# Where the even chunk's values stand while the next unit's keys are projected

## The chip, the cores and the metric

The kernel runs on one core of one Trainium2 chip, in one launch. The metric is the time of one execution on the device in microseconds (us); the time before is the median of three runs.

The engines are named as the profile names them: PE is TensorE's matmul path and PEld its weight loads, DVE is VectorE, ACT is ScalarE, POOL is GpSimd, SP is SyncE, which here only issues DMAs.

## The reference

The reference is a block of three residual layers on x of 8 batches x 1024 tokens x 512 features, all in float32:

```
x = x + 0.5 * ffn(layernorm(x))      # 32 experts, each takes its 8 best tokens of a batch
x = x + attention(layernorm(x))      # the layer that the change is in
x = x + 0.5 * ffn(layernorm(x))
```

The attention has 16 heads of 32 features and is linear and causal:

```
q = exp(x @ Wq.T + bq);  k = exp(x @ Wk.T + bk);  v = x @ Wv.T + bv      # per head
kv = cumsum(k[:, :, None] * v[:, None, :], tokens);  k1 = cumsum(k, tokens)
out = einsum(q, kv) / sum(q * k1);  return out @ Wo.T + bo
```

## The kernel before, in words

**Stages.** The first feed-forward layer streams the experts' weights and lasts until about 820 us in the trace. The attention follows until about 1920, and then the second feed-forward layer streams its weights to the end.

**Tiling of the attention.** A batch has 8 chunks of 128 tokens (c); two chunks make a unit of 256 tokens (u). For batches 0 to 3 (NB0 = 4) the units are projected in the attention, by the generator `project` (L591). For batches 4 to 7 the projections were made beside the first feed-forward layer, and `project_rest` (L630) only scales and corrects them.

**What one unit's projection does.** `project` normalizes two chunks on DVE (L330), turns each with four PE transposes into a PSUM tile ps_aT (L338), and ACT copies each turned chunk to xnT (L339). Then 16 matmuls each form two key tiles ps_k (L610), ACT takes their exponential (L619), and `sum_keys` scans them along the tokens on DVE (L728). There it yields. The queries ps_q (the same lines) follow, and another yield; `times_keys` (L739, on POOL) is the last part.

**What one chunk does.** `attention` (L958) runs over batches and chunks and calls, for an even chunk of batches 0 to 3: `scores` (L785, masked by DVE at L796, by ACT and POOL at L801 and L803), `denominators` (PE L747 into ps_den, reciprocal on DVE L755), the first part of the next unit's projection, `values` (PE L819 into ps_v, copied to va by DVE L826), `turn_keys` (PE transposes L835 into ps_kt, copied to kc by ACT L837), `project_out` of the chunk before (PE L899, added by DVE L906), `spread_denominators` (PE L766), and `attend` (PE L849, L861 and L881). For an odd chunk the next part of the projection, the queries, comes ahead of its values. The values of a chunk read the xnT of that chunk's own unit; the keys at that place belong to the unit after it.

**What sets the order.** In the attention the instructions are recorded in the order of the calls, and a scheduler may move them on each engine; the order of each engine is then fixed, and an engine waits at an instruction until its semaphores are reached. The tiles ps_aT, ps_k, ps_q, ps_v, ps_kt, ps_den, ps_o, ps_n and those of the gate share the pool mm, which has three PSUM banks in the attention; a new tile waits until its bank's last reader has finished. Scores and the spread denominators have a pool of their own (sc).

**The gate.** While the chunks of one batch are worked on, the second layer's gate of the batch before is chosen on DVE in parts (L413 to L431, L518, L541); in the third chunk of batches 1 to 3 these stand among the projection's DVE work.

The lines that matter here:

```
            transposed(t, xnT[:, :, i * P : (i + 1) * P], xc, f"ps_aT_{b}_{c}")
        qkT = open_unit(t, s, b, u)
...
                    if (nb, nu) > (0, 1):
                        of = project_rest if rest else project
                        ahead = of(t, s, nb, nu) if nb < B else iter(())
                        next(ahead, None)
...
                if ("va", b, c) not in s:
                    values(t, s, b, c)
                if not rest:
                    turn_keys(t, s, b, c)
```

Of the kernel before, what the change touches and what calls it, by code (L numbers as in the profile page):

```python
# [20 lines left out]
def kernel(  # L21
# [60 lines left out]
    U = 2  # L82
# [246 lines left out]
    def normalize(dst, xt, mv, rs, c):  # L329
        nc.vector.tensor_scalar(  # L330
            dst, xt[:, c, :], mv[:, c, 0:1], rs[:, c : c + 1], ALU.subtract, ALU.mult
        )

    def transposed(t, dst, src, name):

        ps = t.mm.tile([P, NDC, P], F32, tag="mm", name=name)
        for dc in range(NDC):
            nc.tensor.transpose(ps[:, dc, :], src[:, dc * P : (dc + 1) * P], ident)  # L338
        nc.scalar.copy(dst, ps)  # L339
# [240 lines left out]
    def open_unit(t, s, b, u):  # L580

        un = t.un.tile([P, 4 * NDC * UT], F32, tag=f"un{u % 2}", name=f"un_{b}_{u}")
        qkT = un[:, : 2 * NDC * UT].rearrange("p (o n s) -> p o n s", n=2, s=UT)
        s["q", b, u], s["k", b, u] = qkT[:, :, 0, :], qkT[:, :, 1, :]
        s["k1", b, u], s["rr", b, u] = (
            un[:, i * NDC * UT : (i + 1) * NDC * UT].rearrange("p (o s) -> p o s", s=UT)
            for i in (2, 3)
        )
        return qkT

    def project(t, s, b, u, between=iter(())):  # L591


        xt, mv, rs = s["xt", b]
        xnT = t.n2.tile([P, NDC, UT], F32, tag="xnT", name=f"xnT_{b}_{u}")
        s["xnT", b, u] = xnT
        for i in range(U):
            c = u * U + i
            xc = t.n2.tile([P, D], F32, tag="xc", name=f"xc_{b}_{c}")
            normalize(xc, xt, mv, rs, c)  # L600
            nc.gpsimd.tensor_add(xt[:, c, :], xt[:, c, :], bo_sb)  # L601
            transposed(t, xnT[:, :, i * P : (i + 1) * P], xc, f"ps_aT_{b}_{c}")
        qkT = open_unit(t, s, b, u)
        for n, bias in (("k", bk_sb), ("q", bq_sb)):
            for oh in range(NDC // 2):
                ps = t.mm.tile([P, 2, UT], F32, tag="mm", name=f"ps_{n}_{b}_{u}_{oh}")
                for o in range(2):
                    oc = oh * 2 + o
                    for dc in range(NDC):
                        nc.tensor.matmul(  # L610
                            ps[:, o, :],
                            lhsT=w_sb[n][:, dc, oc * P : (oc + 1) * P],
                            rhs=xnT[:, dc, :],
                            start=(dc == 0),
                            stop=(dc == NDC - 1),
                        )
                for o in range(2):
                    oc = oh * 2 + o
                    nc.scalar.activation(  # L619
                        s[n, b, u][:, oc, :], ps[:, o, :], AF.Exp, bias=bias[:, oc : oc + 1]  # L620
                    )
                next(between, None)
            if n == "k":
                sum_keys(t, s, b, u)
                yield
        yield
        times_keys(t, s, b, u)
        yield
# [95 lines left out]
    def sum_keys(t, s, b, u):  # L724
        k1 = s["k1", b, u]
        before = s.pop(("k1", b, u - 1), None)
        for og in range(NDC):
            nc.vector.tensor_tensor_scan(  # L728
                k1[:, og, :],
                ones.to_broadcast([P, UT]),  # L730
                s["k", b, u][:, og, :],
                0.0 if before is None else before[:, og, UT - 1 : UT],
                ALU.mult,
                ALU.add,
            )

    def times_keys(t, s, b, u):
        qk = t.a1.tile([P, NDC, UT], F32, tag="qk", name=f"qk_{b}_{u}")
        nc.gpsimd.tensor_mul(qk, s["q", b, u], s["k1", b, u])  # L739
        s["qk", b, u] = qk  # L740
# [73 lines left out]
    def values(t, s, b, c):  # L814
        cols = slice(c % U * P, (c % U + 1) * P)
        va = t.a2.tile([P, D], F32, tag="va", bufs=3, name=f"va_{b}_{c}")
        ps = t.mm.tile([P, D], F32, tag="mm", name=f"ps_v_{b}_{c}")
        for dc in range(NDC):
            nc.tensor.matmul(  # L819
                ps,  # L820
                lhsT=s["xnT", b, c // U][:, dc, cols],
                rhs=w_sb["v"][:, dc, :],
                start=(dc == 0),
                stop=(dc == NDC - 1),
            )
        nc.vector.tensor_copy(va, ps)  # L826
        s["va", b, c] = va

    def turn_keys(t, s, b, c):

        cols = slice(c % U * P, (c % U + 1) * P)
        if c < NCH - 1:
            ps = t.mm.tile([P, NDC, P], F32, tag="mm", name=f"ps_kt_{b}_{c}")
            for og in range(NDC):
                nc.tensor.transpose(ps[:, og, :], s["k", b, c // U][:, og, cols], ident)  # L835
            kc = t.a2.tile([P, NDC, P], F32, tag="kc", name=f"kc_{b}_{c}")
            nc.scalar.copy(kc, ps)  # L837
            s["kc", b, c] = kc
# [119 lines left out]
    def attention(t, early, preload):  # L958
# [40 lines left out]
        for _ in project(t, s, 0, 0, begun):  # L999
            pass  # L1000
        ahead = project(t, s, 0, 1, begun)
        next(ahead)
        for _ in begun:
            pass
        last = None
        for b in range(B):
            for c in range(NCH):
# [16 lines left out]
                nb, nu = divmod(b * (NCH // U) + c // U + 1, NCH // U)  # L1024

                rest = NB0 <= nb < B
# [21 lines left out]
                if c % U == 0:  # L1048
# [21 lines left out]
# [3 lines that stand above are left out]
# [5 lines left out]
                    next(ahead, None)  # L1078
                if ("va", b, c) not in s:
                    values(t, s, b, c)  # L1080
                if not rest:
                    turn_keys(t, s, b, c)
                if last is not None:
# [479 lines left out]
    with ExitStack() as stack:  # L1563
        t = open_token_pools(stack, True, early, keep)
        attention(t, early, preload)
# [133 lines left out]
```

## Time and profile before

| what | us |
|---|---|
| median of three runs | 2563.76 |
| lowest and highest run | 2558.55, 2567.12 |
| the profiled execution, its own time | 2561.89 |
| the span of its trace, first to last instruction | 2560.0 |

| stage of the trace, us from its start | PE busy | DVE busy | DMA share |
|---|---|---|---|
| 0 to 830: first feed-forward layer | 741.1 of 830 | 190.2 | 0.96 |
| 904 to 1448: units projected in the attention | 532.5 of 544 | 253.4 | 0.07 |
| 1448 to 1780: units projected ahead | 313.2 of 332 | 246.7 | 0.34 |
| 1980 to 2560: second feed-forward layer | 334.8 of 580 | 48.2 | 0.96 |

A line of the timeline gives the start in us from the span's start, the duration, the engine, the line of the code, the operation with output and inputs, the tile's shape, and the number of instructions merged into the row. In brackets is the engine's idle time just before, and what released it. A wait is put down to the engine whose semaphore came last. The ends of matmuls are modelled, so the start of one group to the start of the next is the safer measure on PE. The granted clock is the share of TensorE's full clock that it was given.

### The profile page before, as it was taken

Reading aid. Unit: us, or ns where it says so; the run is one execution under the profiler, and the core shown is the slowest. Engines: PE = TensorE matmul, PEld = TensorE weight load, DVE = VectorE, ACT = ScalarE, POOL = GpSimd, SP = SyncE. Lnnn points to the kernel's source line nnn. Section 1 sums busy time; section 2 is a strip of 40 time slices with the busy share of each in tenths; the row PEclk is TensorE's granted clock in tenths of the full one; section 3 lists DMA queues with packets and bytes.
Section 4 is the critical chain, followed back from the end, with each engine's and each line's share of the span. In section 5 each row is a group of like instructions: output and inputs, shape, how many; then the busy total and the mean of one; then the engine's idle time right before and its main releaser. Section 6 shows DMA issues by size and latency. Waiting matters only on the chain.

```text
span 2560.0 us, 41819 instructions
## 1 busy us (share of the span) xinstructions
PE 2156.0 (84%) x18679; PEld 1134.8 (44%) x18679; DVE 867.4 (34%) x1495; ACT 498.2 (19%) x965; POOL 377.1 (15%) x345
## 2 busy tenths in 40 slices
PE   8799999999986999999999999999986555555555
PEld 5354544544532666666666655555541111110111
DVE  7311111111111343543544468878850000100002
ACT  6310001000000322322223233443530000000000
POOL 0000000000000112111112235545414000000002
PEclk9899999999997999999999999999987778878777
DMA  7799999999998000001010043243179999999995
GB/s 281 299 426 427 426 428 427 427 427 426 429 428 339 6 1 18 20 31 39 4 61 20 20 164 110 94 147 117 68 280 405 424 427 428 427 428 429 426 428 230
DMA packets 95636, 668.24 MB, mean 261 GB/s; under 512 B 18254, under 2 KB 22606, under 8 KB 58592
## 3 DMA queue, kind: packets, MB, share of 16 engines
q1 hardware_dynamic: 73952, 621.71, 58.9%
q10 hardware_dynamic: 18432, 35.66, 3.6%
q0 software_dynamic: 3072, 8.19, 0.8%
q8 instruction: 147, 2.41, 0.4%
q14 instruction: 33, 0.27, 0.0%
HBM read 614.34 MB, written 48.23 MB: 259 GB/s over the span
## 4 chain that ended last, share of the span: by engine, by line
PE 47%; issue 23%; DMA 16%; DVE 7%; ACT 2%; POOL 1%; POOLq 0%; ACTq 0%; DVEq 0%; SPq 0%
DMA w<-in_w 12%; PE ps_o L899 7%; PE ps_k L610 4%; PE ps_q L610 4%; PE ps_v L819 4%; PE ps_sq L1164 3%; PE ps_sk L1164 3%; PE h_ps L1254 3%; PE p_ps L1277 3%; PE sp L785 2%; PE ps_n L849 2%; DMA pg<-pmT_d,chosen_idx 2%; PE ps_sv L1181 2%; PE ps_n L861 2%; DVE st L314 1%
## 5 line engine op out<-in xcount | busy, mean ns | idle before, releaser
L1254 PE MATMUL h_ps<-w,mT 128*8 128x512 f32 x2048 | 285.9, 692 | 121.8 <-DMA w<-in_w 121.2
L1263 DVE STREAM_TRANSPOSE hs<-h_ps 128x512 f32<-128x512 f32 x64 | 45.9, 717 | 717.8 <-PE h_ps L1254 717.8
L1277 PE MATMUL p_ps<-w,pm 128*32 128x512 f32 x1024 | 173.6, 812 | 135.1 <-DMA w<-in_w 126.8
L899 PE MATMUL ps_o<-wo_sb,at 128*128 128x512 f32 x512 | 236.8, 606 | 1.1 <-ACT rsb L650 1.1
L1254 PEld LDWEIGHTS h_ps<-w,mT 128*8 128x8 f32 x2048 | 50.6, 94 | 332.0 <-issue 195.3
L1277 PE MATMUL p_ps<-w,gl 128*32 128x512 f32 x1024 | 132.5, 650 | 35.5 <-DMA w<-in_w 35.4
L601 POOL TENSOR_TENSOR xt<-xt,bo_sb 128x512 f32<-128x512 f32 x32 | 46.2, 1459 | 765.3 <-PE ps_ocT L338 706.1
L1277 PEld LDWEIGHTS p_ps<-w,pm 128*32 128x32 f32 x1024 | 35.3, 130 | 272.8 <-issue 130.7
L803 POOL TENSOR_SCALAR_AFFINE_SELECT am<-am 128x512 f32<-128x512 f32 x128 | 78.7, 639 | 436.0 <-ACT am L801 291.4
L899 PEld LDWEIGHTS ps_o<-wo_sb,at 128*128 128x128 f32 x512 | 93.5, 192 | 109.2 <-issue 103.4
L314 DVE BATCH_NORM_STATS2 st<-xt 128x6 f32<-128x512 f32 x192 | 128.3, 684 | 4.9 <-DMA xt<-in_x 2.4
L610 PE MATMUL ps_k<-xnT,wk_sb 128*128 128x256 f32 x512 | 115.3, 383 | 10.8 <-ACT xnT L339 10.8
L1270 ACT ACTIVATE pm<-a 128x128 f32<-128x128 f32 x32 | 9.9, 309 | 583.3 <-DVE a L1265 583.3
L1164 PE MATMUL ps_sq<-xcT,wq_sb 128*128 128x256 f32 x512 | 118.6, 388 | 4.1 <-ACT xcT L241 4.1
L1164 PE MATMUL ps_sk<-xcT,wk_sb 128*128 128x256 f32 x512 | 117.4, 385 | 0.0
L1181 PE MATMUL ps_sv<-wv_sb,xcT 128*128 128x512 f32 x256 | 115.6, 599 | 0.0
L819 PE MATMUL ps_v<-wv_sb,xnT 128*128 128x512 f32 x256 | 115.1, 593 | 0.0
L610 PE MATMUL ps_q<-xnT,wq_sb 128*128 128x256 f32 x512 | 115.1, 382 | 0.0
L1164 PEld LDWEIGHTS ps_sq<-xcT,wq_sb 128*128 128x128 f32 x512 | 96.7, 193 | 35.3 <-issue 17.4
L1164 PEld LDWEIGHTS ps_sk<-xcT,wk_sb 128*128 128x128 f32 x512 | 96.8, 192 | 28.0 <-issue 15.4
L610 PEld LDWEIGHTS ps_k<-xnT,wk_sb 128*128 128x128 f32 x512 | 95.8, 190 | 28.4 <-ACT xnT L339 14.6
L610 PEld LDWEIGHTS ps_q<-xnT,wq_sb 128*128 128x128 f32 x512 | 95.9, 190 | 15.7 <-ACT un L619 0.8
(246 smaller groups left out, 2835.3 us busy)
## 6 DMA issues: line engine op xcount, KB each, us to landing
w<-in_w SPq DMA_DIRECT2D x256, 2048.0 KB, 29.3
xt<-in_x SPq DMA_DIRECT2D x31, 1024.0 KB, 8.9
pre<-ahead_d SPq DMA_DIRECT2D x16, 1536.0 KB, 6.4
ahead_d<-ahead_qk ACTq DMA_DIRECT2D x16, 1024.0 KB, 11.5
out<-xt SPq DMA_DIRECT2D x16, 1024.0 KB, 4.7
xs<-in_x ACTq DMA_DIRECT2D x16, 512.0 KB, 18.2
ahead_d<-ahead_v ACTq DMA_DIRECT2D x16, 512.0 KB, 11.3
pm<-pm SPq DMA_DIRECT2D x16, 128.0 KB, 2.4
```

Source lines behind the costliest of these rows:

```text
L314: nc.vector.bn_stats(st, xt[:, c, :])
L610: nc.tensor.matmul(ps[:, o, :], lhsT=w_sb[n][:, dc, oc * P : (oc + 1) * P], rhs=xnT[:, dc, :], start=(dc == 0), stop=(dc == NDC - 1),)
L785: nc.tensor.matmul(sp[r // 2][:, r % 2, og, :], lhsT=kT[hr, og, cols], rhs=qT[hr, og, cols], start=True, stop=True,)
L803: nc.gpsimd.affine_select(out=am[1][:, i, :, :], in_=am[1][:, i, :, :], pattern=[[0, NDC], [1, P]], compare_op=ALU.is_ge, fill=0.0, base=0 ...
L819: nc.tensor.matmul(ps, lhsT=s["xnT", b, c // U][:, dc, cols], rhs=w_sb["v"][:, dc, :], start=(dc == 0), stop=(dc == NDC - 1),)
L849: nc.tensor.matmul(ps[hr, og, :], lhsT=va[:, (og * HG + r) * HD : (og * HG + r + 1) * HD], rhs=am[r // 2][:, r % 2, og, :], start=(og == 0 ...
L861: nc.tensor.matmul(ps[hr, og, :], lhsT=kv[hr, og, :], rhs=qT[hr, og, cols], start=False, stop=True, skip_group_check=True,)
L899: nc.tensor.matmul(ps, lhsT=at[:, oc, :], rhs=w_sb["o"][:, oc, :], start=(oc == 0), stop=(oc == NDC - 1),)
L1164: nc.tensor.matmul(ps[:, o, :], lhsT=w_sb[w][:, dc, oc * P : (oc + 1) * P], rhs=xcT[:, dc, :], start=(dc == 0), stop=(dc == NDC - 1),)
L1181: nc.tensor.matmul(ps, lhsT=xcT[:, dc, i * P : (i + 1) * P], rhs=w_sb["v"][:, dc, :], start=(dc == 0), stop=(dc == NDC - 1),)
L1254: nc.tensor.matmul(h[32 * j : 32 * j + B, :], lhsT=mT[:, dc, e, :], rhs=w1h[dc // 2][:, dc % 2, j * 512 : (j + 1) * 512], start=(dc == 0), ...
L1277: nc.tensor.matmul(pp[32 * j : 32 * (j + 1), :], lhsT=gl4[e % 4][:, q, :, :].rearrange("p i b -> p (i b)"), rhs=w2h[q // (NU // 2)][:, q % ...
```

## The change

`project` gets one more yield, between the turning of the tokens and the keys. Where the attention used to advance it once in an even chunk, it now advances it once before the values and once after them; ahead of the loop, the unit (0, 1) is advanced twice, so nothing moves there. For units projected ahead (`rest`) nothing changes. It concerns the units (0, 2) to (3, 3), 14 in all.

```diff
@@ project, after the turning of the unit's two chunks
             transposed(t, xnT[:, :, i * P : (i + 1) * P], xc, f"ps_aT_{b}_{c}")
+        yield
         qkT = open_unit(t, s, b, u)
@@ attention, ahead of the loop
         ahead = project(t, s, 0, 1, begun)
         next(ahead)
+        next(ahead)
         for _ in begun:
@@ attention, in the loop over chunks
                 if ("va", b, c) not in s:
                     values(t, s, b, c)
+                if c % U == 0 and not rest and (nb, nu) > (0, 1):
+                    next(ahead, None)
                 if not rest:
                     turn_keys(t, s, b, c)
```

## The prediction, made before the changed kernel ran

> **What bounds the kernel.** I read the page's busy times first, then a table of busy time by stage, then the waits of TensorE (PE) in the stage that the change touches, then the timeline of one unit there, engine by engine.
>
> ```profile
> PE 2156.0 (84%) x18679; PEld 1134.8 (44%) x18679; DVE 867.4 (34%) x1495; ACT 498.2 (19%) x965; POOL 377.1 (15%) x345
> ```
>
> The share over the whole span mixes stages, so the stage table decides. Its columns are the stretch and its length, busy time (and count) of PE, PEld, DVE, ACT and POOL, the granted PE clock, the DMA share and GB/s.
>
> ```profile
> 904.00:1448.00 544.00, 532.54 (x5229) 363.20 (x5230) 253.38 (x395) 148.22 (x276) 109.78 (x99) 1.00 0.07 23
> 1448.00:1780.00 332.00, 313.22 (x4346) 187.40 (x4348) 246.66 (x375) 131.43 (x254) 154.40 (x125) 0.97 0.34 117
> 1980.00:2560.00 580.00, 334.76 (x1936) 63.39 (x1928) 48.21 (x90) 8.35 (x27) 21.45 (x22) 0.78 0.96 405
> ```
>
> The 14 units that the change reorders are projected between 904 and 1448. There PE is busy 532.5 of 544 us at full clock, DVE 47% and DMA 7%: PE is the path, and only its 11.5 idle us can be won without removing work. The waits in that stage (who waited for whom: us in total, times, longest) say whose they are:
>
> ```profile
> PE ps_k L610 <- ACT xnT L339: 9.8, 14, 0.7
> PE ps_ocT L338 <- DVE oc L918: 1.7, 1, 1.7
> PE ps_aT L338 <- DVE xt L308: 0.9, 2, 0.7
> ```
>
> Fourteen waits, one for each reordered unit: the first key matmul waits for ScalarE (ACT) to copy the turned tokens out of PSUM. One unit on PE (start, duration, engine, line, what, count, idle before and its releaser):
>
> ```profile
> 1024.91 0.64 PE L747 MATMUL ps_den<-qk,hsum 128*32 128x256 f32 x8
> 1025.48 1.09 PE L338 MATMUL ps_aT<-ident,xc 128*128 128x128 f32 x8
> 1027.30 7.17 PE L610 MATMUL ps_k<-xnT,wk_sb 128*128 128x256 f32 x32 [0.73 <-ACT xnT L339]
> 1034.31 3.60 PE L819 MATMUL ps_v<-wv_sb,xnT 128*128 128x512 f32 x8
> 1037.74 0.60 PE L835 MATMUL ps_kt<-ident,un 128*128 128x128 f32 x4
> ```
>
> The reader is to see that the values (ps_v) stand behind the keys though they read the unit before (its xnT is long done). The same stretch on ACT and DVE:
>
> ```profile
> 1025.15 1.02 ACT L801 COPY am<-sp 128x1024 f32<-128x1024 f32 x1 [9.28 <-PE sp L785]
> 1026.17 1.07 ACT L339 COPY xnT<-ps_aT 128x512 f32<-128x512 f32 x2
> 1034.51 0.84 ACT L619 ACTIVATE un<-ps_k,bk_sb 128x256 f32<-128x256 f32 x2 [2.61 <-PE ps_k L610]
> ```
>
> ```profile
> 1026.15 1.75 DVE L755 RECIPROCAL rd<-ps_den 128x256 f32<-128x256 f32 x1
> 1037.94 0.69 DVE L826 COPY va<-ps_v 128x512 f32<-128x512 f32 x1 [1.53 <-PE ps_v L819]
> ```
>
> **The bubble's size.** PE's ends overlap what follows: four transposes (ps_kt) show 0.60 us, but the next group starts 0.44 after them. So the idle column is short by 0.16 each time, and the bubbles come to 9.8 + 14 x 0.16 = 12.0 us.
>
> **The change, part by part.** The order of instructions in the built program, with the waits that it carries, shows what moves. On PE, in 14 units, the four value matmuls stand ahead of the sixteen key matmuls; nothing else. On DVE the copy va (L826) stands ahead of the four scans (L728), in three units also ahead of L426, L431 and L518. The orders of ACT, POOL and SP are unchanged, so no DMA is issued earlier or later in its queue, and nothing is added or removed: busy time changes by 0.
>
> *When can the values start?* They need a PSUM bank of the three of pool mm, and in the built program their first matmul waits for ACT, one count short of what the first key matmul waits for: for the first of the two xnT copies, which frees the first transposes' bank. One copy lasts 0.586 us (minimum and median of its line), and before the change PE starts 0.05 after the second one's end (1026.17 + 1.07 = 1027.24, keys at 1027.30). So the values start where the first copy ends, and the gain of a unit is the duration shown for both copies less 0.59. I read the 14 pairs: seven show 1.07 us (0.48 each, 3.4), two 1.13 or 1.14 (0.55, 1.1), four 1.29 (0.70, 2.8). In the first unit (0, 2) the first copy has ended before the last transposes; these start at 906.08, take 0.44, and the keys started at 907.40, so 0.85 (less the 0.03 that I leave). **Sum: 8.1 us.** What stays is 12.0 - 8.1 = 3.9 us of waiting for the first copy.
>
> *What is late next?* The values take 3.43 us from start to start (1034.31 to 1037.74), the second copy ends 0.5 to 0.7 us after the values start, so the keys find it done: 0. The second key group takes the bank of the denominators, released by the reciprocal L755; it starts 3.43 + 3.5 us after the values, and the worst reciprocal ends 4.5 us after the old key start (unit 1233, below): 0. The turning of the keys (ps_kt) now takes the values' bank and waits for va. That copy is queued behind DVE's backlog, worst where the top-k of the gate runs:
>
> ```profile
> 1236.74 1.75 DVE L755 RECIPROCAL rd<-ps_den 128x256 f32<-128x256 f32 x1
> 1240.89 1.12 DVE L541 TENSOR_SCALAR chosen_idx<-chosen_idx 32x8 uint32<-32x8 uint32 x1
> 1241.93 1.21 DVE L426 SCALAR_TENSOR_TENSOR pm<-pm,lg 32x1024 f32<-32x1024 f32 x1
> ```
>
> There va takes L426's place at 1241.9 and ends at 1242.6; ps_kt comes at 1234.00 - 0.55 + 10.44 = 1243.9. Margin 1.3 us, so 0. If DVE were 2 us later, the three such units would lose 0.7 each, 2 us in all. Queued behind ps_kt on PE is the output projection, so such a wait would be paid in full.
>
> The later key exponentials come 3.43 us later against PE, and two scans with them. ACT then copies kc (L837) behind two exponentials (0.84), about 0.4 us later than now; its reader, the ps_kv matmuls, stand 6 us behind (1043.71). The scans end about 2.0 us after ps_kt starts; the next DVE work (L906) waits for the output projection 4.1 us after that start. Both are covered: 0. In the top-k units L906's margin is 1 us.
>
> *Does it reach the end?* Between 1448 and 1780 PE is still busy 94%, and the last stage runs on its weight stream (DMA 0.96), whose first big batch is issued at 1867 behind the attention's last batch. Everything after is released by work on this chain, so I carry it over in full.
>
> [...] The keys' start 0.05 us after the second copy is a data wait, since the copy writes what they read. [...]
>
> **The rivals.**
> - *Bank gap* (0.08): the values get no bank before the second copy, or the order on the chip is not that of the build. For: three banks only, all three drawn just before. Against: the wait on the first copy. 0 us: 2563.8.
> - *Whole bubble* (0.10): the values run straight behind the transposes. For: they have no data to wait for. Against: the same bank. -12.0: 2551.8.
> - *Given back* (0.16): PE meets a later wait, at ps_kt or L906 in the top-k units, or in the stages after 1448 where DVE is busy 74%. For: margins of 1.0 to 1.3 us. Against: those engines are released by PE itself. About half remains: -4, 2559.7.
> - *Slower: the bank of the denominators* (0.04). Three banks in plain rotation would hand the values the bank of ps_den, free when the reciprocal ends. It decides as soon as that end lies behind the old key start, and it does in all 14 units: by 0.6 (1027.90 against 1027.30) in six and 0.3 in the first, 2.3 in four, 3.8 and twice 4.5 in the top-k ones, in sum about 26 plus 0.05 for each: +26.7, 2590.5. Against: before the change the keys were next in that rotation, and started 0.6 us ahead of that end.
>
> **How the numbers follow.** The profiled execution took 2561.89 us, of which 2560.0 is the span; less 8.1 it would be 2553.8. The median of the three runs is 1.87 us above it, so the forecast stands at 2563.76 - 8.1 = **2555.7**, chance 0.62. The three runs spread by 8.6 us, and half-clock stretches (0.97 between 1448 and 1780) fall elsewhere in each execution; a median of three may be off by 3. The range 2550 to 2563 takes in that, the whole bubble and the bank gap. About 0.3% (7.7 us, below 2556.1) is what a measurement of this kernel can tell from no change, and my forecast lies right on it. So faster: 0.62 x 0.55 + 0.10 x 0.95 + 0.16 x 0.1 = 0.45; slower 0.04; the rest, 0.51, within.
>
> **What would show it.** The fourteen waits of ps_k on xnT vanish, and shorter ones of ps_v on xnT, 0 to 0.25 us, stand in their place; the values start 0.05 us after the first copy's end; from there to ps_kt stays 10.44 us; PE's idle time in the stage falls by 8. It is wrong if ps_v waits for DVE, if ps_kt waits for va, or if the stretch from 904 to the last unit shortens by 8 and the end does not.

## The result, and the profile after

The changed kernel takes 2555.22 us in the median of seven runs (2551.45 to 2559.55), the kernel before, run beside it, 2564.97 (2558.55 to 2568.60). The ratio is 0.9964, with a 95% interval of 0.9954 to 0.9974: 9.2 us faster (6.7 to 11.8); the two medians themselves lie 9.75 apart. Seven more runs of it later gave 0.9970 (0.9958 to 0.9981), 7.7 us. The forecast was 2555.7, or 8.1 us.

The busy times of the page of the changed kernel come first, then its table by stage. The columns are those of the tables of before.

```profile
PE 2165.0 (85%) x18679; PEld 1142.9 (45%) x18679; DVE 865.8 (34%) x1495; ACT 497.1 (19%) x965; POOL 373.8 (15%) x345
```

```profile
904.00:1440.00 536.00, 532.43 (x5224) 361.87 (x5225) 251.58 (x395) 145.64 (x272) 106.56 (x99) 1.00 0.07 23
1440.00:1772.00 332.00, 315.56 (x4349) 191.02 (x4347) 244.37 (x371) 129.57 (x251) 153.51 (x124) 0.96 0.33 114
```

The reader is to see that no engine has other work: the counts over the whole span are those of before. PE does the same 532.4 us in a stretch that is 8 us shorter. Over the whole span its busy time is 9.0 us more than before, with as many instructions; the granted clock is a half for 416.4 us of this execution and for 396.0 of the one before, so the sum over the span says nothing about the change. The PE waits from 880 to 1440 (who waited for whom: us in total, times, longest) say which idle time went:

```profile
PE ps_v L820 <- ACT xnT L339: 1.7, 7, 0.2
PE ps_ocT L338 <- DVE oc L919: 1.7, 1, 1.7
PE ps_aT L338 <- DVE xt L308: 0.9, 2, 0.7
```

The 14 waits of the keys (9.8 us) are gone, and seven short ones of the values stand in their place. The same unit as in the prediction, on PE, then on ACT and DVE:

```profile
1024.54 1.09 PE L338 MATMUL ps_aT<-ident,xc 128*128 128x128 f32 x8
1025.87 3.70 PE L820 MATMUL ps_v<-wv_sb,xnT 128*128 128x512 f32 x8 [0.24 <-ACT xnT L339]
1029.41 7.07 PE L611 MATMUL ps_k<-xnT,wk_sb 128*128 128x256 f32 x32
1036.32 0.60 PE L836 MATMUL ps_kt<-ident,un 128*128 128x128 f32 x4
```

```profile
1025.23 1.07 ACT L339 COPY xnT<-ps_aT 128x512 f32<-128x512 f32 x2
```

```profile
1029.61 0.69 DVE L827 COPY va<-ps_v 128x512 f32<-128x512 f32 x1 [1.82 <-PE ps_v L820]
1037.02 1.39 DVE L729 TENSOR_TENSOR_SCAN un<-ones,un,un 128x256 f32<-128x256 f32 x2 [1.99 <-ACT un L620]
```

One copy lasts 0.59 us, so the first ends at 1025.82. The values start at 1025.87; the second copy ends at 1026.31, three us ahead of the keys, which find it done. In 13 of the 14 units the values start 0.05 us after the first copy's end; in the first the copy is done before the last transposes, and the values follow these.

**One execution is a poor witness for the end.** The profiled executions took 2561.89 us before and 2559.55 after (the slowest of its seven), only 2.3 less. I split each trace at two starts of the turning of keys (ps_kt): the one just ahead of the 14 units (888.58 in the trace of before) and the one of the last unit's odd chunk (1473.23). The first two rows are of before, the other two of after:

```profile
888.58 0.60 PE L835 MATMUL ps_kt<-ident,un 128*128 128x128 f32 x4
1473.23 0.60 PE L835 MATMUL ps_kt<-ident,un 128*128 128x128 f32 x4
```

```profile
889.88 0.60 PE L836 MATMUL ps_kt<-ident,un 128*128 128x128 f32 x4
1466.14 0.60 PE L836 MATMUL ps_kt<-ident,un 128*128 128x128 f32 x4
```

Between them lies all that the change touches, and in what follows this is "the stage". It takes 584.65 us before and 576.26 after: 8.4 us less. The other 6.1 us were lost elsewhere: 1.3 ahead of it, where the attention began later, 3.8 between it and the last ps_kt (1875 before), and 0.9 behind. In the part with the 3.8 the instructions are the same, but the granted clock falls to a half in stretches of 3.4 us (half-clock stretches, below) that lie differently in each execution: from 1450.6 to 1872.5 they come to 20.5 us before and 30.7 after. A kernel whose 14 units run exactly as before (the sixth below) shows 37.5 us of them, and 5.3 us more in that part than the execution of before. In the ten traces kept here that part lasts from 402.1 us, where it has the least half clock (the 20.5 of before), to 409.5, where it has the most (41.0, kernel 2 once more). So the 3.8 need no cause in the change, and the runs together, which average over this, agree with the whole 8.4.

### The profile page after: what moved, and what is told of

The parts are those of the page before. It is cut to its first block, busy times and chain, and to the rows that moved or that the text cites. A ratio compares the mean times of both kernels' runs of the same rounds, so it can differ in the third digit from the quotient of the medians.

```text
span 2557.7 us, 41819 instructions
## 1 busy us (share of the span) xinstructions
PE 2165.0 (85%) x18679; PEld 1142.9 (45%) x18679; DVE 865.8 (34%) x1495; ACT 497.1 (19%) x965; POOL 373.8 (15%) x345
## 4 chain that ended last, share of the span: by engine, by line
PE 48%; issue 23%; DMA 16%; DVE 7%; ACT 1%; POOL 1%; POOLq 0%; ACTq 0%; DVEq 0%; SPq 0%
DMA w<-in_w 12%; PE ps_o L900 7%; PE ps_q L611 4%; PE ps_v L820 4%; PE ps_k L611 4%; PE ps_sk L1168 3%; PE ps_sq L1168 3%; PE h_ps L1258 3%; PE p_ps L1281 2%; PE ps_n L850 2%; PE ps_sv L1185 2%; PE sp L786 2%; DMA pg<-pmT_d,chosen_idx 2%; PE ps_n L862 2%; DVE st L314 1%
## 6 DMA issues: line engine op xcount, KB each, us to landing
ahead_d<-ahead_qk ACTq DMA_DIRECT2D x16, 1024.0 KB, 11.5
```

## The experiments

My theory after the result: the gain is made on PE alone; the values run while ACT makes the second copy, and what is left of the bubble is the wait for the PSUM bank that the first copy frees. The rivals: the gain comes from DVE, which copies the values ahead of the scans; it would come with any work put in the bubble; or the bubble was a lack of PSUM from the start. The table gives each kernel's ratio to the kernel before, run beside it; the difference that follows (the median of the kernel before, in that comparison, times the ratio less 1); the difference of the stage; and how many half-clock stretches of 3.4 us that stage has more than in the trace of before, which has two, at 896.5.

| kernel | ratio (95%) | us | stage, us | half-clock stretches more |
|---|---|---|---|---|
| changed kernel | 0.9964 (0.9954 to 0.9974) | -9.2 | -8.4 | 0 |
| changed kernel, once more | 0.9970 (0.9958 to 0.9981) | -7.7 | -8.4 | 0 |
| 1: copy of the values behind the scans | 1.0017 (1.0007 to 1.0028) | +4.4 | +5.5 | 1 |
| 2: values in the scores' bank | 0.9938 (0.9924 to 0.9951) | -15.9 | -14.4 | 0 |
| 2, once more | 0.9944 (0.9929 to 0.9960) | -14.4 | -11.4 | 2 |
| 3: denominators as the filler | 0.9994 (0.9981 to 1.0006) | -1.5 | +0.9 | 3 |
| 4: values in the denominators' bank | 1.0104 (1.0087 to 1.0121) | +26.7 | +26.7 | 7 |
| 5: scores' bank, copy behind the scans | 0.9961 (0.9948 to 0.9974) | -10.0 | -12.7 | 1 |
| 6: before, keys in the scores' bank | 1.0000 (0.9991 to 1.0009) | 0.0 | 0.0 | 0 |

The stage agrees with the medians to within 3 us in every row, and where the stretches are as many as before, to within 1.5. So what is gained or lost in the 14 units reaches the end, as far as these intervals, of 2 to 4 us to each side, can tell.

**1: DVE's copy put back behind the scans.**

```diff
-        nc.vector.tensor_copy(va, ps)
+        if late:
+            s["vp"] = va, ps
+        else:
+            nc.vector.tensor_copy(va, ps)
...
                 if c % U == 0 and not rest and (nb, nu) > (0, 1):
                     next(ahead, None)
+                if "vp" in s:
+                    tc.keep_in_program_order(nc.vector.tensor_copy(*s.pop("vp")))
```

> The changed kernel, with DVE's copy of the even values put back behind the four scans in the 14 units; PE keeps the new order, values ahead of keys. My theory: the 8 us come from PE, which runs the values while ACT makes the second copy of the turned tokens; DVE's order gains nothing. Then the keys still start about 3.4 us after the values and no wait on the turned tokens longer than 0.25 us comes back. The new order of DVE costs a little of its own: the turning of the keys takes the bank of the first keys, and the output projection waits for ACT's exponentials of the second keys, which end about 1.04 us after the turning starts, where PE is ready after about 0.77: 0.3 us in each of 14 units, +4 us on the changed kernel, so about 4 to 5 us below the kernel before (ratio 0.998). Rival: the gain comes from the copy standing ahead of the scans on DVE, and the kernel is back at the time of before (ratio 1.000 or above).

It came out 4.4 us slower than before. By the time alone this is the rival's ratio (1.000 or above), but the trace gives it another reason. The values start as in the changed kernel, their waits are the same 1.7 us in seven units, and 10.44 us later ps_kt starts. But behind that PE's order is another one: half of the spread denominators now stand ahead of the output projection. I put that down to the scheduler, which finds the bank of the values free later and the banks of pool mm in another rotation; no run shows that reason apart. Their group in the stretch from 904 to 1440 (busy us, mean ns of one, idle before), of the changed kernel and then of this one:

```profile
L767 PE MATMUL ps_rr<-rd,hrep 32*128 32x256 f32 x104 | 9.3, 427 | 0.0
```

```profile
L767 PE MATMUL ps_rr<-rd,hrep 32*128 32x256 f32 x104 | 18.2, 426 | 0.0
```

The same 104 matmuls, 13 units, occupy 8.9 us more, 0.68 a unit. Eight together take 0.65 us to the next group; two groups of four take 0.63 each (in the unit at 1038.34). Against the changed kernel the way from the even chunk's ps_kt to the next one is 0.81 us longer in eight units, 0.40 in two, 1.40 in three (in the one at 1037.81 the next scores are split too), and 2.39 in the last, into which a half-clock stretch at 1462.7 falls: 13.9 in all, as much as the stage lost. So the run spoke of PE's order, not of DVE's, and could not decide its question.

**5: the same question without the side effect.** With the values in the scores' bank (2, below) the copy can be put behind the scans and PE's order stays the same to the instruction. The diff is those of 1 and 2 together.

> The kernel with the values in the scores' bank, with one thing more: DVE copies the even values behind the four scans again, as before the change. The order of PE, ACT, POOL and SP is the same to the instruction as with the values in the scores' bank; only DVE's order differs. The run with the late copy in the old bank could not tell what DVE's order is worth, because its banks rotated differently and the spreading of the reciprocals and the scores were split on PE. My theory: the gain is made on PE alone; the copy ends about 2.8 us after the turning of the keys starts, the next reader of its bank comes 5.3 us after it, and DVE's next work waits for the output projection at 4.1: ratio 0.993 to 0.995, the same as with the early copy, and about 0.2% below the changed kernel. Rival: half or more of the gain came from the copy standing ahead of the scans: ratio 0.997 or above.

The stage gained 12.7 us where kernel 2 gained 14.4. Of the 1.7 between them, 1.5 come from a half-clock stretch at 1120.8 in the unit whose ps_kt starts at 1112.46 (23.92 us to the next ps_kt, where kernel 2 takes 22.45), 0.2 from everything else. So DVE's order is worth next to nothing, and the gain is PE's. The time itself (0.9961) is higher than I expected. Its interval begins at 0.9948, where those of kernel 2 lie from 0.9924 to 0.9960: by the time alone the two can't be told apart for sure, nor this one from the changed kernel. What the trace shows of the stage doesn't explain a difference of 4 to 6 us, so that part stays open (there were five runs).

**2: another bank for the values.**

```diff
-        ps = t.mm.tile([P, D], F32, tag="mm", name=f"ps_v_{b}_{c}")
+        if aside:
+            ps = t.sc.tile([P, 2, 512], F32, tag="sp1", name=f"ps_v_{b}_{c}")[:, 0, :]
+        else:
+            ps = t.mm.tile([P, D], F32, tag="mm", name=f"ps_v_{b}_{c}")
```

> The changed kernel, with the even values of the 14 units written to the second PSUM tile of the scores, which is free when ACT has copied the masked scores, ahead of the first copy of the turned tokens. My theory: what is left of the bubble in the changed kernel (3.9 us by the forecast's sum) is the wait for the bank that the first copy frees. With another bank the values start straight behind the turning, the waits of the values on the turned tokens go from 7 to about none, and the kernel is 3.5 to 3.9 us faster than the changed one: about 12 us, or 0.47%, below the kernel before (ratio 0.9953, where the changed kernel measured 0.9964). Rival: the values start 0.05 us after the first copy for another reason than the bank (PE's own latency behind the transposes, or data), and nothing changes against the changed kernel. Second rival: the second half of the reciprocals' spreading, which takes the scores' tile later in the unit, then waits for DVE's copy of the values; a wait of PE on that copy would show at its line and take the gain back.

It beats both kernels, by more than I expected. One unit on PE:

```profile
1022.28 1.10 PE L338 MATMUL ps_aT<-ident,xc 128*128 128x128 f32 x8
1023.21 3.60 PE L823 MATMUL ps_v<-wv_sb,xnT 128*128 128x512 f32 x8
1026.65 7.07 PE L611 MATMUL ps_k<-xnT,wk_sb 128*128 128x256 f32 x32
1033.56 0.60 PE L839 MATMUL ps_kt<-ident,un 128*128 128x128 f32 x4
```

The values follow the turning 0.93 us after its start, without a wait; in the changed kernel it was 1.33. From the values to ps_kt it takes 10.34 us, not 10.44 (1026.65 to 1033.56 is 6.91 in both; the values' own part is 3.44 instead of 3.54). A wait on PE thus cost 0.10 us more than its idle time here. (I call this the restart.) And in the first unit, whose two chunks are turned with a wait between them, the first two value matmuls run inside that wait, and its ps_kt comes 0.79 us sooner behind the one before it. So what was left in the changed kernel was 3.9 us of waiting, 1.3 of restarting (13 x 0.10) and 0.8 in the first unit: 6.0; the stage shows 14.4 - 8.4 = 6.0. The bank was the cause of all of it. No wait of PE on the copy va shows, so the second rival did not come true either.

> The kernel with the even values in the scores' bank once more, since it had five runs and its advantage over the changed kernel is 6 us or less of 2555. My theory: from the turning of the keys ahead of the 14 units to that of the last, it is 14.4 us shorter than the kernel before, as in its first trace, and all of it reaches the end: ratio 0.993 to 0.9955. Rival: its first ratio of 0.9938 was partly luck, and the version is no better than the changed kernel's 0.9964 to 0.9970.

The second time the ratio was 0.9944. The stage gained 11.4 us in that execution, with two more half-clock stretches in it (three instead of two at 895 to 905, and one at 1120.3), which at 1.5 us each bring back the 14.4. Both intervals lie almost wholly below the two of the changed kernel.

> The changed kernel itself once more, beside the two above on one chip, so that the bank's worth is read against it there. My theory: ratio to the kernel before 0.996 to 0.997, and in its trace the reciprocal of the last unit again 8 us earlier against that of the first than in the kernel before. Rival (part of the gain is given back behind the stage, as the single profiled execution seemed to say with 2.3 us): ratio 0.998 or above.

The stage gained 8.4 us again, to 0.1, and the end 7.7 by the ratio.

**3: another filler.**

```diff
                 if c % U == 0:
-                    if not rest:
+                    if not rest and (nb, nu) <= (0, 1):
                         denominators(t, s, b, c // U)
...
                 if c % U == 0 and not rest and (nb, nu) > (0, 1):
+                    denominators(t, s, b, c // U)
                     next(ahead, None)
```

It stands in the changed kernel with its values put back behind the keys.

> The kernel before with its values behind the keys, as before the change, but the eight matmuls of the denominators (0.57 us from start to start in the unit at 1024.91) put between the turning of the next unit's tokens and its keys in the 14 units. My theory: a filler gains only if the copies of the turned tokens don't shift with it. Here they do not start earlier when the transposes do, because ACT is still copying the masked scores until 1026.17 in that unit; PE comes to the turning 0.57 us sooner, waits for the same copies and finds the keys at the same time: 0 to -2 us against the kernel before (ratio 0.999 to 1.000). Rival: any work of PE in the bubble is won in full, 14 x 0.57 = 8 us (ratio 0.997). Second rival: the reciprocal on DVE starts 0.5 to 1 us later and what reads the denominators' bank, the second group of keys, waits for it in the three top-k units: +1 us each, +3 us.

No difference that can be measured. PE, ACT and DVE in the unit:

```profile
1026.86 1.09 PE L338 MATMUL ps_aT<-ident,xc 128*128 128x128 f32 x8
1027.88 0.64 PE L748 MATMUL ps_den<-qk,hsum 128*32 128x256 f32 x8
1029.14 7.17 PE L611 MATMUL ps_k<-xnT,wk_sb 128*128 128x256 f32 x32 [0.62 <-ACT xnT L339]
```

```profile
1027.10 1.01 ACT L802 COPY am<-sp 128x1024 f32<-128x1024 f32 x1 [9.28 <-PE sp L786]
1028.01 1.08 ACT L339 COPY xnT<-ps_aT 128x512 f32<-128x512 f32 x2
```

PE turns the tokens earlier, but ACT is still copying the masked scores. The copies keep their place behind that, and the keys start 0.05 us after the second, as before. The 0.57 us put into the bubble had stood ahead of the turning, beside the same copy of the scores, and PE waits on as before. From each ps_kt of the 14 units to the next it takes 0.1 to 0.4 us less than before, 2.3 us in the twelve intervals without a half-clock stretch: a third of the 12 x 0.57 that the rival promised. The stage came out 0.9 longer because three such stretches fell into it, two in the first unit (the clock is a half until 911.3 there, and until 903.3 in the trace of before) and one at 1293.6. The second rival, keys waiting for a later reciprocal, didn't show. So not any filler did: work from ahead of the turning won these 2.3 us, and work from behind the keys won 8.4 (the changed kernel), which is 0.60 a unit, the time of a copy.

**4: the slower rival, built.**

```diff
-        ps = t.mm.tile([P, UT], F32, tag="mm", name=f"ps_den_{b}_{u}")
+        both = s["both"] = t.mm.tile([P, D], F32, tag="mm", name=f"ps_den_{b}_{u}")
+        ps = both[:, :UT]
...
-        ps = t.mm.tile([P, D], F32, tag="mm", name=f"ps_v_{b}_{c}")
+        if shared:
+            ps = s["both"]
+        else:
+            ps = t.mm.tile([P, D], F32, tag="mm", name=f"ps_v_{b}_{c}")
```

> The changed kernel, with the even values of the 14 units written into the PSUM tile of the denominators, so that they must wait for DVE's reciprocal. One key matmul stands ahead of them on PE. This builds the slower rival of the forecast to see whether its mechanism and price are real. By that sum each unit stalls until the reciprocal's end: against the kernel before, about 0.2 us in six units, 1.9 in four, 3.4 and twice 4.1 in the top-k ones, +20 us (about 2584, ratio 1.008), with waits of the values on DVE of that sum in the trace of PE. Rival: DVE's reciprocal moves up with PE, since it waits for the denominators and not for DVE's backlog, and the price is under half of that (ratio below 1.004).

The values bear the name ps_den here. Their wait from 904 to 1475, and one unit with the gate's top-k:

```profile
PE ps_den L824 <- DVE rd L757: 14.5, 7, 3.4
```

```profile
1241.03 1.13 PE L611 MATMUL ps_k<-xnT,wk_sb 128*128 128x256 f32 x4 [0.68 <-ACT xnT L339]
1245.57 6.66 PE L824 MATMUL ps_den<-wv_sb,xnT 128*128 128x512 f32 x8 [3.41 <-DVE rd L757]
1252.06 6.21 PE L611 MATMUL ps_k<-xnT,wk_sb 128*128 128x256 f32 x28
```

The mechanism is real: PE waits for the reciprocal in the seven units where it ends late (1.26 us four times, 2.70 once, 3.41 twice). In the other seven the key matmul in front, four rows of 0.97 us together, covers it, more than the 0.44 that I had allowed. A unit with a wait of 1.26 and a full clock takes 1.52 us longer than before, which is the wait, the 0.16 of the modelled ends and the 0.10 of a restart. The waits and seven times 0.26 come to 16.3 us, under my 20. The rest is something I had not counted: eight value matmuls take 6.49 us to the next group here (1245.57 to 1252.06), against 3.44 without a wait. The granted clock (0.50, behind the busy times of PE, PEld, DVE, ACT and POOL) is a half there:

```profile
1244.72:1251.55 6.83, 5.99 (x7) 2.52 (x8) 6.45 (x9) 1.24 (x2) 3.77 (x2) 0.50 0.00 0
```

In or just behind five of the seven waits there are such stretches, seven of 3.4 us in all, and they are left with 26.7 - 16.3 = 10.4 us, 1.5 each.

**6: was it PSUM from the start?**

```diff
-                ps = t.mm.tile([P, 2, UT], F32, tag="mm", name=f"ps_{n}_{b}_{u}_{oh}")
+                if n == "k" and oh == 0 and (b, u) > (0, 1):
+                    ps = t.sc.tile([P, 2, 512], F32, tag="sp1", name=f"ps_{n}_{b}_{u}_{oh}")
+                    ps = ps[:, 0, :].rearrange("p (o s) -> p o s", s=UT)
+                else:
+                    ps = t.mm.tile([P, 2, UT], F32, tag="mm", name=f"ps_{n}_{b}_{u}_{oh}")
```

This is the kernel before with that edit alone.

> The kernel before with one thing changed: the first key group of the 14 units is written to the second tile of the scores, which is free before the turned tokens are copied. The order on all engines is that of before. This asks whether the 12 us in front of the keys were a wait for PSUM. My theory: it is a wait for data, since the keys read what the second copy writes; the bank changes nothing, the waits of the keys on the turned tokens stay at 9.8 us in 14 units, ratio 0.999 to 1.001. [...]

Nothing moved, and the wait is the old one to the digit:

```profile
PE ps_k L614 <- ACT xnT L339: 9.8, 14, 0.7
```

The bank itself was free: in kernel 2 the values run in it from 1023.21, before the first copy has ended (1022.98 + 0.59 = 1023.57). So the keys waited for data. The other bank helped only where something without that data stood in front: by 14.4 us of the stage in kernel 2, by 0.0 here.

## Why the prediction was right

- **What bounds.** Right. PE's idle time in the stretch fell from 11.5 to 3.6 us, by 7.9 where 8 was forecast, and the busy time stayed.
- **When the values start.** Right: 0.05 us after the first copy in 13 units. The pairs of copies gave 7.3 for these 13, and from ps_kt of the first unit to that of the last the trace is 7.33 us shorter. The first unit gave 1.05, forecast as 0.82. Sum 8.1, measured 8.4 in two traces.
- **What is late next.** Right. ps_kt comes 10.44 us behind the values. In the top-k units of the changed kernel va ends 1.2 us ahead of it (1239.13 against 1240.30); I had said 1.3. L906 (now L907), whose margin I gave as 1 us, cost nothing either.
- **Does it reach the end.** Right over all runs. My own test for it (the stretch shortens by 8 and the end does not) would have condemned it from the one trace; it should have asked for the medians. That the median, 2555.22, lies 0.5 us from the forecast is in part luck: the kernel before came out 1.2 us above the three runs that I had started from, and the interval of the gain is 2.6 us to each side. No run shows the 0.3% (7.7 us) that my chances took as what a measurement can tell from no change; seven runs of each kernel left 2.6 us, 0.1%, to each side.
- **The bubble's size.** Too small. I had 12.0, from idle time and 0.16 for each end. The rival that fills it whole is worth 14.4 us, not 12.0, because a restart costs 0.10 a unit (1.3) and the first unit offers more than I had counted: 0.2 of it in the changed kernel, 0.8 with the free bank.
- **The slower rival.** Its price of 26.7 is what kernel 4 shows, but by chance: its units lose 16.3 by waiting, and the lowered clock, which my sum did not have, makes up the rest.
- **The gap's cause.** I had taken the gap for a data wait, and what the change leaves of it for a wait for a bank. Kernel 6 (ratio 1.0000, the waits 9.8 us in 14 units as before) shows that the gap as it stood was not for want of a bank; kernel 2 (a stage 6.0 us shorter than the changed kernel's) shows that the bank was the cause of the 6 us that the change left. One gap had two causes, one behind the other.

## What to carry to other kernels

When a saturated engine waits again and again for another one's copy (here PE for ACT, 9.8 us in 14 units), look for work behind the wait that needs none of that data, and read which PSUM bank that work would get. Here the bank kept it waiting in place of the data (1.7 us in seven listed waits of the changed kernel's values, and 6.0 us by what the other bank won in kernel 2), and a bank that was free earlier, one of the scores', gave the rest. Work taken from ahead of the copy's own inputs won little where the copy was held by its engine: 2.3 us, a third of its time. Compare two profiled executions stage by stage, between instructions that both have, before believing a difference of their ends.

## What the hardware showed that I had not expected

- **Short waits often came with a lowered clock.** In kernel 4, waits of 1.26 us came with a half-clock stretch of 3.4 us in two of four units (it starts within the wait or less than 2 us behind it), and the longer ones (2.70 and twice 3.41 us) each time. The wait of 1.65 us at the attention's start (1.7 in the list of waits, ps_ocT) is followed by two to four such stretches in all ten traces, the 14 waits of 0.7 us before the change by none. So a wait's length alone doesn't decide: behind the stage (to 1880 us) the 1.38 us in front of ps_m come with one in 26 of 30 cases in the ten traces, the 1.32 to 1.43 in front of ps_kt in 14 of 30, and the 1.0 to 1.6 in front of ps_rr in none of 26. Kernel 4 apart, the stage has four more stretches, one each in kernels 1, 3, 5 and 2 once more. They began without such a wait, 1.7 to 2.5 us after the start of the same 16 matmuls of 32x32 (ps_pmT); but 27 groups of these stand in the stage in the nine traces other than kernel 4's, so most bring none, and that the small matmuls are the cause is a guess. A stretch cost about 1.5 us (kernel 5 against kernel 2: 23.92 against 22.45). What starts one, no run shows.
- **Eight matmuls on 32 rows took what four did.** The eight of ps_rr, listed with 0.43 us each, took 0.65 us together, and 0.63 for each four alone. So splitting this group cost as much as doubling it: 8.9 us of PE's busy time in 13 units.
